# A four-layer graph network on one core: where layer 0's finished rows are split into word planes

## The chip, the core and the metric

The kernel runs on one core of a Trainium2 chip. A core has five instruction streams: PE (TensorE, matrix products; its weight loads are listed as PEld), DVE (VectorE), ACT (ScalarE), POOL (GpSimd) and SP (SyncE, which here only issues DMAs). Each executes its own list of instructions in order and waits on semaphores for the others. The metric is the device time of one launch in microseconds (us), lower is better. The time before the change is the median of three runs.

## The reference

A graph of 2708 nodes with 512 features goes through four layers; after each layer the result is added to its input and every row is normalised. The change touches layer 0 and the way from layer 0 to layer 1:

```python
x = _layernorm(x + _L0_gnn_ref(x, adj, W_nb, b_nb, W_line, b_line, 64))

# _L0_gnn_ref: mean over at most the first 64 neighbours of each node
keep = Ab & (jnp.cumsum(Ab.astype(jnp.int32), axis=1) <= neibor_num)
nb_mean = (keep.astype(X.dtype) @ X) / jnp.maximum(cnt, 1.0)
xj = leaky_relu(nb_mean @ W_nb.T + b_nb)
xi = leaky_relu(X @ W_line.T + b_line)
return xi + jnp.where(cnt > 0, xj, 0)
```

Layer 1 takes the finished rows x, multiplies them by two folded weight matrices and by the full adjacency. Layers 2 and 3 are graph attention; nothing of them is touched.

## The kernel before

The rows are handled in 22 tiles of 128 (the last, tile 21, has 20 rows; the name LAST). One work buffer for masks, `maskT`, holds the transposed adjacency of all tiles in a small format. Instructions of each engine are put in order at build time by a scheduler, which goes by the order in which the program creates them and by its own estimate of when each is ready; an instruction whose buffer is not yet free is put later. On the chip each engine keeps that order. The program ties some instructions behind others by hand (`issue_after`).

Layer 0 has two stages. In the first (to about 190 us in the profile) y = x W_nb is made for all tiles and kept on chip in two parts (yH, yL), and r0 = x W_line + b_line is written to DRAM (`r0_dram`). The second stage, the one that matters here, runs from about 190 to 486 us. It computes, block by block, the sums of neighbours keep @ y. A block is up to four row tiles; the blocks are taken in the order 20-21, 0-3, 4-7, 8-11, 12-15, 16-19 (`cuts`). For each block the loop goes over j = 0 to 21:

- `kept` (L470, ACT) makes `kT`, the slice of the mask for this j and this block, in two rotating buffers.
- L608 (PE) multiplies it with yH and yL of tile j, for each of the block's tiles: up to eight matmuls per j.
- `next(todo)` in two of three steps j runs one step of `finish` for the block before.
- `next(both)` in each step j runs one step of `other_masks`, and when that is used up of `weights1`, and then of `vectors`.

At the end of a block ACT scales its sums into `us` (L621).

`finish` has two steps per tile. The first fetches the tile's r0 and x (`fetched`, L205, issued by SP) and does on DVE: add a bias to u (L524), leaky (L229) on u and on r0, and r0 += x (L528). The second does on DVE u = u * has + r0 (L530) and the layer norm of u (L121 to L128, with one power on POOL, L126); then POOL stores the row tile to `x1_dram` (L532), and `store_words` (L149, L150) copies u once more, split into a plane of low and a plane of high 16-bit words, and POOL stores this copy to `x1_words`. In the next loop these words are read back by transposing DMAs (L155), tile by tile.

The fetched tiles lie in three rotating buffers with the name "rows" (pool `ahead`). The r0 and the x of a tile are two of them. The same three serve `weights1`, which fetches eight tiles of layer 1's weights, transposes them on PE (L139) between the sums and multiplies them (L299), and the transposing reads of the next loop. The memory for the word planes is the r0 tile itself, so its buffer is in use from the fetch of r0 until the store of the words has landed.

`other_masks` makes the last eight tiles of the mask. For each: a DMA of adjacency rows (L312, POOL), a count on ACT (L317), four running counts on DVE (`place`, L323 and L326), a transposing DMA on SP (`turn`, L344), and, some steps j later, signs on ACT into `maskT` (L349). These signs stand in ACT's list between kT instructions. Each mask takes 11 steps j.

The two rotating buffers with the name "u" (pool `sm`) hold r0 results in the first stage, and u results in the loop after this stage (L642). In this stage one of them is `acc`, a sum that `weights1` builds; the other has no use.

Of the kernel before, what the change touches and what calls it, by code (L numbers as in the profile page):

```python
# [10 lines left out]
F32 = mybir.dt.float32  # L11
# [9 lines left out]
P = 128  # L21
D = 512
# [10 lines left out]
def kernel(  # L33
# [18 lines left out]
    def rows(t):  # L52
        return min(P, N - t * P)
# [38 lines left out]
    x1_words = dram.tile([N, 2 * D], U16, name="x1_words")  # L92
# [51 lines left out]
    def store_words(room, dst, t, u):  # L144

        if t == LAST:
            return
        words = room.bitcast(U16)
        nc.vector.tensor_copy(words.rearrange("p (h c) -> p h c", h=2), u.bitcast(U16).rearrange("p (c h) -> p h c", h=2))  # L149
        nc.gpsimd.dma_start(dst[t * P:t * P + P, :], words)  # L150
# [86 lines left out]
    with ExitStack() as phase:  # L237
# [23 lines left out]
        sm = phase.enter_context(tc.tile_pool(name="l01", bufs=2))  # L261
# [44 lines left out]
        cuts = [(b, min(b + 4, NT)) for b in range(0, NT, 4)]  # L306
        cuts = cuts[-1:] + cuts[:-1]
# [48 lines left out]
        with ExitStack() as ph:  # L356
# [65 lines left out]
            for t in range(NT):  # L422
# [27 lines left out]
                u = sm.tile([P, D], F32, name="u")  # L450
# [12 lines left out]
        with ExitStack() as ph:  # L463
# [56 lines left out]
            def finish(ts_, us):  # L520
                for t in ts_:
                    n, u = rows(t), us[t]
                    r0, x0 = fetched(r0_dram, t, n), fetched(x, t, n)
                    nc.vector.tensor_add(u[:n], u[:n], b_nb[:n])  # L524
                    leaky(u[:n], u[:n])
                    with tc.issue_after(low.ins):
                        leaky(r0, r0)
                        nc.vector.tensor_add(r0, r0, x0)  # L528
                    yield
                    nc.vector.scalar_tensor_tensor(u[:n], u[:n], has[:n, t:t + 1], r0, op0=OP.mult, op1=OP.add)  # L530
                    layer_norm(sm, u[:n], n, u[:n])
                    nc.gpsimd.dma_start(x1_dram[t * P:t * P + n, :], u[:n])  # L532
                    store_words(r0, x1_words, t, u)
                    yield

            wnb, wself = [], weight2
            acc = sm.tile([P, D], F32, name="u")
            bias1 = sm.tile([P, D], F32, name="bias1", bufs=1)  # L540

            def weights1():
# [55 lines left out]
            for i, b in enumerate(cuts):  # L598
                ts_ = range(*b)
# [28 lines left out]
            for t in range(NT):  # L628
# [12 lines left out]
                u = sm.tile([P, D], F32, name="u")  # L641
# [3 lines left out]
        with ExitStack() as ph:  # L645
            st = ph.enter_context(tc.tile_pool(name="l1b", bufs=2))
            for t in range(NT):
# [12 lines left out]
                u = sm.tile([P, D], F32, name="u")  # L660
# [36 lines left out]
    cuts = [-((-NT * i) // nb) for i in range(nb + 1)]  # L697
# [938 lines left out]
```

## Time and profile before

| what | value |
|---|---|
| median of three runs | 2902.19 us (2900.64 to 2906.04) |
| the profiled execution's own time | 2901.7 us |
| its span in the profile | 2899.6 us |
| mean granted clock of PE | 0.994 |
| L608, sums of layer 0 with yH, busy | 173.4 us, 418 matmuls |
| L608, sums with yL, busy | 166.1 us, 418 matmuls |
| L866, DVE, attention weights, busy | 1132.1 us |
| L1067, PE, attention sums, busy | 894.2 us |

The profile is one execution taken by the hardware profiler. Its span runs from the first to the last recorded instruction; the execution's own time is 2.1 us longer. A line of a timeline has the start in us from the span's start, the duration in us, the engine, the line of the program, the operation, what it writes and reads with sizes, how often, and in brackets how long the engine stood idle before it and what released it. On SP the instruction's duration is that of issuing the DMA. Matmul ends are modelled, and neighbouring ones overlap; intervals between starts are more reliable than durations. A list of waits has the waiting engine and line, the one waited for, total us, times, and the longest.

### The profile page before, as it was taken

The numbers are of one execution on the slowest core, as the hardware profiler recorded it, in microseconds if no ns is written. First come the engines' busy times: TensorE is split into PE (matmuls) and PEld (weight loads), VectorE is DVE, ScalarE is ACT, GpSimd is POOL, SyncE is SP. The second block draws the span as 40 slices with busy tenths as digits, with TensorE's granted clock in tenths as the row PEclk, the third lists the DMA queues.
The fourth block names the chain that finished last, engine by engine and source line by source line (L and its number), as shares of the span: only waits on it lengthen the run. The fifth ranks groups of instructions, "written<-read, shape, count | busy, mean of one in ns | idle before, by whom it ended". The sixth has DMA issues, their size and how long they took to land. (4 is left out here: it accounts for less than half of the span.)

```text
span 2899.6 us, 35696 instructions
## 1 busy us (share of the span) xinstructions
PE 2810.6 (97%) x13910; PEld 1556.4 (54%) x13910; DVE 2009.6 (69%) x2386; ACT 1525.3 (53%) x1749; POOL 269.2 (9%) x436
## 2 busy tenths in 40 slices
PE   9999889999999999999999999999999999999998
PEld 5457666448887443444466433434475555555565
DVE  6867647644334999999978999999953535345343
ACT  4646533223234999999965999999951000000011
POOL 2112211101120000000012000000201010100001
PEclk9999999999999999999999999999999999999999
DMA  7745537524324011111143111110161000000000
GB/s 170 151 101 116 151 104 178 160 63 124 112 91 89 27 37 36 35 46 39 38 141 126 38 37 36 40 57 34 35 160 62 4 26 15 26 15 16 15 15 28
DMA packets 203669, 202.64 MB, mean 70 GB/s; under 512 B 126838, under 2 KB 151739, under 8 KB 203491
## 3 DMA queue, kind: packets, MB, share of 16 engines
q1 hardware_dynamic: 170646, 127.60, 16.7%
q0 software_dynamic: 21840, 68.46, 8.1%
q10 hardware_dynamic: 11004, 4.22, 0.6%
q8 instruction: 111, 1.82, 0.3%
q14 instruction: 68, 0.55, 0.1%
HBM read 137.90 MB, written 55.66 MB: 67 GB/s over the span
## 5 line engine op out<-in xcount | busy, mean ns | idle before, releaser
L866 DVE SCALAR_TENSOR_TENSOR e<-v_bc,ucol,maskT 128x1408 f32<-128x1408 f32 (+3 forms) x798 | 1132.1, 1484 | 316.8 <-PE pn L1267 308.3
L895 ACT ACTIVATE c<-e,bcol 128x1300 fp8e4<-128x1300 f32 (+2 forms) x688 | 956.7, 1412 | 61.5 <-DVE e L866 16.5
L1067 PE MATMUL po<-e,R 128*64 128x512 f32 (+3 forms) x4224 | 894.2, 548 | 25.7 <-DVE e L866 23.3
L1067 PEld LDWEIGHTS po<-e,R 128*64 128x64 f32 (+1 forms) x4224 | 333.7, 136 | 553.2 <-issue 389.7
L1267 PE MATMUL pn<-e,R 128*128 128x512 f32 (+1 forms) x1008 | 396.3, 557 | 0.8
L1267 PEld LDWEIGHTS pn<-e,R 128*128 128x128 f32 x1008 | 177.5, 190 | 195.9 <-issue 181.5
L1196 ACT ACTIVATE w<-pl,b 128x256 f32<-128x256 f32 (+1 forms) x88 | 41.0, 466 | 365.6 <-PE pl L1194 365.6
L608 PE MATMUL acc<-yH,kT 128*128 128x512 f32 x418 | 173.4, 415 | 15.5 <-ACT kT L470 14.2
L126 POOL TENSOR_TENSOR ln_rs<-ln_rs,half 128x1 f32<-128x1 f32 (+1 forms) x88 | 54.9, 624 | 1363.5 <-DVE ln_rs L125 1347.8
L787 PE MATMUL pm<-w,xT 128*128 128x264 f32 (+1 forms) x704 | 164.1, 388 | 2.8 <-issue 0.9
L608 PE MATMUL acc<-yL,kT 128*128 128x512 f32 x418 | 166.1, 397 | 0.0
L658 PE MATMUL acc<-yH,mf 128*128 128x512 f32 x418 | 162.7, 389 | 0.0
L658 PE MATMUL acc<-yL,mf 128*128 128x512 f32 x418 | 162.6, 389 | 0.0
L1194 PE MATMUL pl<-lin 128*128 128x256 f32 (+1 forms) x704 | 152.9, 371 | 0.6 <-DVE lin L1096 0.6
L1219 PE MATMUL pl<-lin,w 128*128 128x512 f32 x336 | 150.8, 593 | 0.0
L1194 PEld LDWEIGHTS pl<-lin 128*128 128x128 f32 x704 | 129.3, 190 | 31.2 <-issue 15.8
L787 PEld LDWEIGHTS pm<-w,xT 128*128 128x128 f32 (+1 forms) x704 | 129.7, 190 | 28.6 <-ACT xT L141 3.1
L655 ACT CAST mf<-maskT 128x1024 fp32r<-128x1024 fp8e4 (+1 forms) x66 | 64.5, 978 | 149.0 <-PE acc L658 144.4
L299 PE MATMUL pm<-w,xT 128*128 128x512 f32 x288 | 130.0, 594 | 1.6 <-DVE yL L276 1.0
L470 ACT ACTIVATE kT<-maskT 128x512 fp32r<-128x512 fp8e4 (+1 forms) x132 | 77.3, 592 | 100.4 <-PE acc L608 100.1
L967 PE MATMUL pd<-c,parts_c 128*12 128x384 fp8e4 (+2 forms) x2688 | 128.3, 307 | 0.0
L299 PE MATMUL pm<-weight,xT 128*128 128x512 f32 (+1 forms) x256 | 117.4, 602 | 2.6 <-DVE u L642 2.6
(278 smaller groups left out, 2780.1 us busy)
## 6 DMA issues: line engine op xcount, KB each, us to landing
v_bc<-v_dram SPq DMA_DIRECT2D x16, 704.0 KB
rows<-in_x_dram SPq DMA_DIRECT2D x42, 256.0 KB
x_dram<-u POOLq DMA_DIRECT2D x42, 256.0 KB, 2.4
v_bc<-v_dram SPq DMA_DIRECT2D x16, 650.0 KB
m<-in_adj_dram POOLq DMA_DIRECT2D x13, 677.0 KB, 7.8
r_dram<-u POOLq DMA_DIRECT2D x21, 256.0 KB, 3.6
rows<-r_dram SPq DMA_DIRECT2D x21, 256.0 KB
x_words<-rows POOLq DMA_DIRECT2D x21, 256.0 KB, 3.6
```

Of the source, the lines that this page charges most:

```text
L299: order(nc.tensor.matmul(pm[:m], xT[:, k, :m], w[:, k, :], start=(k == 0), stop=(k == KD - 1)))
L470: made = nc.scalar.activation(kT[:, :w], maskT[:, j, b[0] * P:b[0] * P + w], AF.Relu, scale=-1.0)
L608: nc.tensor.matmul(pa[t], kT[:, (t - b[0]) * P:(t - b[0] + 1) * P], y(j), start=(j == 0 and y is yH), stop=(j == LAST))
L658: nc.tensor.matmul(pa, mf[:, j - g0, :], y(j), start=(j == 0 and y is yH), stop=(j == LAST))
L787: nc.tensor.matmul(pm[a][:m, :D // 2 + heads], xT[:, k, :m], w[:, k, a, :D // 2 + heads], start=(k == 0), stop=(k == KD - 1))
L866: self.made = nc.vector.scalar_tensor_tensor(e[:, :w], v[:, :w], ucol[:, j, h:h + 1], maskT[:, j, c0:c0 + w], op0=OP.max, op1=OP.mult)
L895: nc.scalar.activation(c[:, :w], e[:, :w], AF.Sigmoid, bias=bcol[:, j, h:h + 1], scale=STEP, saturate=False)
L967: pe(nc.tensor.matmul(p[32 * g:32 * g + 12, :c1 - c0], parts_c[:, j, h, :], c[:, c0:c1], start=(i == 0 and h == hs[0]), stop=(i == NT - 1 ...
L1067: pe(nc.tensor.matmul(po[i][HO * k:HO * k + HO, :c1 - c0], R2[at, j, h * HO:(h + 1) * HO], e[at, a:a + c1 - c0], start=(i_ == 0), stop=(i_ ...
L1194: nc.tensor.matmul(pl[:, :w], self.lin1[:, k, f * P:(f + 1) * P], h[:, k, :w], start=(k == 0), stop=(k == KD - 1))
L1219: nc.tensor.matmul(pl[:n], gT[:, f, (t - t0) * P:(t - t0) * P + n], self.lin2[:, f, :], start=(f == 0), stop=(f == KF - 1))
L1267: nc.tensor.matmul(pn[k][:, :w], R2[at, j, k * P:(k + 1) * P], e[at, :w], start=(j == 0), stop=(j == NT - 1))
```

## The change

Two lines are edited. A second tile of the name "u" is taken beside `acc` for the whole stage, `words`. `finish` gives it to `store_words` as the place for the word planes, except for the tiles of the last block (16 to 19), which are finished in the loop after this stage and still use r0's own memory. So 17 tiles (20 and 0 to 15) share one buffer for their words; tile 21 has no words.

```diff
@@ finish
                     layer_norm(sm, u[:n], n, u[:n])
                     nc.gpsimd.dma_start(x1_dram[t * P:t * P + n, :], u[:n])
-                    store_words(r0, x1_words, t, u)
+                    store_words(r0 if ts_ == range(*cuts[-1]) else words, x1_words, t, u)
                     yield
...
             wnb, wself = [], weight2
-            acc = sm.tile([P, D], F32, name="u")
+            acc, words = (sm.tile([P, D], F32, name="u") for _ in range(2))
             bias1 = sm.tile([P, D], F32, name="bias1", bufs=1)
```

`store_words` itself, unchanged:

```python
words = room.bitcast(U16)
nc.vector.tensor_copy(words.rearrange("p (h c) -> p h c", h=2), u.bitcast(U16).rearrange("p (c h) -> p h c", h=2))
nc.gpsimd.dma_start(dst[t * P:t * P + P, :], words)
```

## The prediction

> **What bounds the kernel now.** I read the page first, for the engine that sets the span, then the waits of TensorE (PE) inside the one stage that the change touches, then backwards along the queues that cause those waits: ScalarE (ACT), SP, VectorE (DVE), SP again. From the page, busy us and share by engine:
>
> ```profile
> PE 2810.6 (97%) x13910; PEld 1556.4 (54%) x13910; DVE 2009.6 (69%) x2386; ACT 1525.3 (53%) x1749; POOL 269.2 (9%) x436
> ```
>
> From the list of PE's waits between 222 and 490 us (waiting engine and line, who was waited for, us in total, times, longest):
>
> ```profile
> PE acc L608 <- ACT kT L470: 18.0, 12, 6.8
> PE ps_tr L139 <- DMA rows<-in_L_gnn_W_self_dram: 4.8, 1, 4.8
> PE acc L608 <- ACT u L621: 1.3, 2, 0.6
> ```
>
> PE is busy 97% of the span, so time is won only where PE stands still. In this stage (the masked sums of layer 0) it stands still for about 24 us. PE's timeline names the long gaps (start, duration, instruction, idle time before it and releaser):
>
> ```profile
> 324.65 0.80 PE L608 MATMUL acc<-yH,kT 128*128 128x512 f32 x1 [3.34 <-ACT kT L470]
> ...
> 353.75 5.28 PE L608 MATMUL acc<-end,kT 128*128 128x512 f32 x12 [6.78 <-ACT kT L470]
> ...
> 375.58 0.68 PE L608 MATMUL acc<-yH,kT 128*128 128x512 f32 x1 [3.10 <-ACT kT L470]
> ...
> 391.36 1.12 PE L139 MATMUL ps_tr<-ident,rows 128*128 128x128 f32 x4 [4.82 <-DMA rows<-in_L_gnn_W_self_dram]
> ```
>
> I call them A, B, C and D: 3.34 + 6.78 + 3.10 + 4.82 = 18.04 us. After each of them PE is also slow for a while. The table by stretch gives length, busy time of PE, PEld, DVE, ACT and POOL, and then the granted clock (PEclk): 0.54 after A, 0.69 after B, and 1.00 in a quiet stretch after D:
>
> ```profile
> 324.60:328.20 3.60, 3.54 (x9) 2.83 (x10) 2.76 (x6) 2.10 (x4) 2.53 (x4) 0.54 0.91 135
> 353.70:361.80 8.10, 8.00 (x22) 5.48 (x23) 4.22 (x8) 5.90 (x11) 0.53 (x1) 0.69 0.53 183
> ...
> 400.00:408.00 8.00, 8.00 (x32) 5.24 (x31) 0.00 (x0) 2.50 (x5) 0.00 (x0) 1.00 0.14 43
> ```
>
> Matmuls of this stage start 0.227 us apart in undisturbed stretches. After A, 8 intervals took 3.46 us instead of 1.81 (1.65 lost); after B, 22 took 8.13 instead of 4.99 (3.14 lost); after C, 10 took 3.97 instead of 2.27 (1.70 lost); after D, four transposes, eight sums and eight product matmuls took 7.62 us against 5.33 for the same group ten microseconds later (2.29 lost). Together 8.8 us, so the four gaps cost 26.8 us.
>
> Why are they there? A, B and C wait for kT, which ACT makes; ACT's timeline shows it stuck, ahead of kT, on a mask transpose that arrives late:
>
> ```profile
> 352.12 1.06 ACT L349 ACTIVATE maskT<-weight 128x1024 fp8e4<-128x1024 bf16 x1 [8.60 <-DMA weight<-spare]
> ```
>
> That is B; the same instruction waited 5.15 us before A and 4.36 us before C. The transposes (L344) left SP at 317.85, 346.20 and 368.68 us, each within 0.2 us of DVE's last L326 on that mask. So DVE's scans of the mask were late, and DVE's timeline shows why, here before A:
>
> ```profile
> 301.07 0.69 DVE L528 TENSOR_TENSOR rows<-rows 128x512 f32<-128x512 f32 x1 [4.52 <-DMA rows<-in_x_dram]
> 307.17 0.69 DVE L229 SCALAR_TENSOR_TENSOR rows<-rows 128x512 f32<-128x512 f32 x1 [5.41 <-DMA rows<-r_dram]
> 307.89 0.69 DVE L528 TENSOR_TENSOR rows<-rows 128x512 f32<-128x512 f32 x1
> 308.50 1.56 DVE L323 TENSOR_TENSOR_SCAN w<-w,over 128x677 bf16<-128x677 bf16 x1
> ```
>
> The scan (L323) of a mask that had been counted by 295 us begins at 308.50, behind two row fetches. And the fetches were late because SP could not issue them. The longest entry of SP's waits between 183 and 560 us, and one fetch on its timeline:
>
> ```profile
> SPq L205 <- DMA x_words<-rows: 67.2, 16, 12.6
> ...
> 331.57 0.33 SPq L205 DMA_DIRECT2D rows<-in_x_dram  x1
> ```
>
> POOL sent tile 4's words store at 327.29; SP's next fetch goes at 331.57, when that store has landed. The circle is closed: a "rows" buffer is held until the words made in it are in DRAM, the fetch into it goes late, DVE stands, the scan, the transpose, the sign and kT are late, PE stands.
>
> **What the Trainium skill says.** "TensorE: Matmul & The Clock Gate", section "HAM oscillation — how this bites in real kernels": idle gaps of more than about 3.4 us drop PE to half clock. The trace agrees: 0.43 us between matmuls instead of 0.227 after A, B and C, even after C's 3.10 us. "Perfetto Trace Analysis", section "DMA Instruction — SWDGE (GPSIMD)": the profiled end of such a DMA is the end of descriptor generation, not of the movement. The trace agrees: a words store occupies POOL for 0.54 us and lands 3.5 us after its issue (median between 300 and 390 us) or 5.2 us (between 183 and 300). "Perfetto Trace Analysis", section "Optimization Strategy": a repeated bubble on the engine that should be saturated can mean that there are too few buffers for the next tile; A to C repeat once per mask and end in a buffer wait.
>
> **The change part by part.** (1) The copy L149 stays one DVE instruction of 0.68 us; only its destination differs, for tile 20 and tiles 0 to 15 (17 copies). The store on POOL and its bytes stay. Cost 0. The buffer was the idle second one of "u" until the next loop's first u at 493 us, about 30 us after tile 15's words left POOL (462.24). Cost 0.
>
> (2) A row buffer comes free after L530, not after the store has landed. For tile 2, L530 ends at 283.1, while the words left POOL at 290.48 and landed 3.5 to 5.2 us later: 11 to 13 us earlier. For tile 3 it is 292.6 against 296.85 + 4.3 = 301.1. For tile 0 it is 265.4 against 278.53. So the waits of DVE at L528 and L229 shrink: 5.16 + 4.52 + 5.41 us between 276 and 308, 3.72 + 4.39 + 3.63 us between 330 and 359.
>
> (3) A new wait: with one buffer, the copy of a tile must wait until the tile before's words have landed. Of the four copies of a block only the first two stand close, 270.84 and 273.16 (and 326.11 and 328.43); the next is 16.0 and 6.7 us later (13.7 and 6.7). The first store is issued at 272.02; landed after 3.5 to 6.5 us, the second copy starts at 275.5 to 278.5, so it waits 2.4 to 5.4 us; I take 4. The third and fourth wait for 0 to 2; I take 0. Behind the waiting copy on DVE stand the scans of the next mask, and behind those SP's transpose, ACT's signs and PE. On POOL the words store waits with the copy, and the next power (L126) or mask load behind it by as much.
>
> Now the gaps. A: its mask's scans start after about 10 us of fetch waits (4.52 + 5.41); those gone, the transpose leaves some 8 us or more earlier, and ACT's wait was 5.15. A goes: 3.34 + 1.65 = 5.0. C is the same case one block later (4.39 + 3.63 against 4.36 on ACT): 3.10 + 1.70 = 4.8. D: the W_self fetch left SP at 388.70, when L528 of tile 11 was done; tile 10's and 11's rows move up by about 9 us (tile 10's second fetch, at 381.09, waited for tile 8's store; L530 of tile 8 ends near 371.6). PE needed the tile at 386.5. D goes: 4.82 + 2.29 = 7.1.
>
> B is the tight one. Its mask shares DVE with the finishing of four tiles. A deadline can be read from the block before: it starts at 261.49, its transpose leaves at 293.21 and costs PE 0.52 us, so 293.21 - 0.52 - 261.49 = 31.2 us after a block's start is early enough. B's block starts at 303.74; DVE's work from 317.63 to 346.05 is 28.4 us with 3.72 of fetch wait in it, so 24.7 without. It can begin 0.9 us after the block's start, as it does in the block before (the last L326 ends at 262.39). 0.9 + 24.7 + the words wait of 2.4 to 5.4 = 28 to 31 us, just inside. I leave 3 us of B's 9.9 standing (2 of idle, 1 of slow clock), since nothing is spare: 6.9 gained.
>
> Sum: 5.0 + 6.9 + 4.8 + 7.1 = 23.8 us. Everything after 490 us is PE-bound with its own order and moves up as a whole. The span was 2899.6 us; the profiled execution's own time, 2901.7, lies 2.1 around it and 0.5 below the median 2902.19. 2902.2 - 23.8 = 2878.4 us.
>
> **The rivals.** (a) The new wait takes half back: copies wait 5 to 6 us per block ahead of a scan, B stays (9.9) and C comes back in part (2): gain 12, 2890 us. For: only 0 to 3 us spare in B's block. Against: 15.1 and 11.7 us of DVE waits go. Chance 0.12. (b) Nothing to be measured: the order on the engines was laid out around the old waits, and ACT's signs stay late for another reason, for instance a transpose queued on SP behind a row fetch that waits for L530. L344 at 262.52 and the end of L530 at 265.4 are only 3 us apart. Gain 0 to 5, 2900 us. Chance 0.09. (c) Slower: three copies per block each stand a whole landing of 6.5 us ahead of the scans, 19.5 us against the 15.1 and 11.7 removed. Then scans are later than before by 4.4 and 7.8 us, PE idles by these 12.2, and about 4 of slow clock follow: 2918 us. It decides from the point where the words waits of a block exceed some 12 to 15 us. Against it: two of the three spacings are 6.7 us or more. Chance 0.08. (d) More: B goes whole (3) and the two waits of 1.79 and 1.17 us at 465 and 470, where x1's first transposed words (SP, 457.70) are late on ACT, go too, since tiles 12 to 15 finish sooner: gain 30, 2872 us. Chance 0.16.
>
> **How the numbers follow.** The forecast has 0.55 (gain 18 to 28, 2874 to 2884), (a) 0.12, (b) 0.09, (c) 0.08, (d) 0.16. About 0.2% (5.8 us) is what a measurement of this kernel can tell from no change. Faster: 0.55 + 0.12 + 0.16 = 0.83; same 0.09; slower 0.08. The range runs from 2869 (all of A to D, the 3 us of late words and their slow clock) to 2898 (a gain of 4); (c), part of (b) and a little beyond (d) are left out, together not quite 2 in 10.
>
> **What would show it.** In the new profile SP's wait for the words store is gone from L205; DVE's waits at L528 and L229 in 262 to 360 us fall from 26.8 us to under 10; ACT no longer waits for the transposes by more than 2 us; PE's gaps A, C and D are absent, and PEclk stays near 1.0 from 305 to 432 us. A new line shows DVE's L149 waiting for the words DMA, some 2 to 5 us per block. I am wrong if that wait is over 12 us per block, if the transposes on SP stand behind a fetch, or if PE still waits for kT with the fetches on time.

## The result, and the profile after

The changed kernel takes 2885.65 us (median of 5 runs, 2884.27 to 2889.62); beside it on the same chip the kernel before takes 2904.49 us (2900.64 to 2906.83). The ratio is 0.9939, with a 95% interval from 0.9924 to 0.9953: 18.8 us less, where 23.8 were forecast, at the lower edge of the forecast's own band of gains (18 to 28). The profiled execution took 2884.27 us, with a span of 2882.5; the spans differ by 17.1 us.

PE is as much the engine that sets the time as before (busy us, share of the span, instructions, from the page of the changed kernel):

```profile
PE 2806.0 (97%) x13910; PEld 1553.3 (54%) x13910; DVE 2008.4 (70%) x2386; ACT 1525.4 (53%) x1749; POOL 267.1 (9%) x436
```

The list of PE's waits between 222 and 490 us has lost over 60% of the waiting for kT (18.0 us before) and the whole of the waiting for W_self (the L299 waits belong to the loop after this stage, 2.30 us of them at 489.35):

```profile
PE acc L608 <- ACT kT L470: 6.8, 8, 3.3
PE pm L299 <- DVE yL L276: 2.7, 2, 2.3
PE pm L568 <- ACT w L560: 1.7, 1, 1.7
PE acc L608 <- ACT u L621: 0.9, 2, 0.6
```

PE's timeline shows what is left of the long gaps. There are two, and they are not both leftovers: the first is in a block that had none of over 0.6 us before.

```profile
300.33 4.61 PE L608 MATMUL acc<-end,kT 128*128 128x512 f32 x12 [2.23 <-ACT kT L470]
...
346.53 5.49 PE L608 MATMUL acc<-end,kT 128*128 128x512 f32 x12 [3.30 <-ACT kT L470]
```

A clean account uses no busy times, only the start of L621, with which ACT ends each block's sums. Us from one such start to the next:

| stretch | before | after | gain | forecast |
|---|---|---|---|---|
| start to first L621 | 220.49 | 219.06 | 1.43 | 0 |
| sums of tiles 0 to 3 | 40.29 | 40.30 | -0.01 | 0 |
| sums of tiles 4 to 7 | 42.25 | 45.08 | -2.83 | 0 |
| sums of tiles 8 to 11 | 55.34 | 46.70 | 8.64 | 11.9 (A and B) |
| sums of tiles 12 to 15 | 71.99 | 59.70 | 12.29 | 11.9 (C and D) |
| sums of tiles 16 to 19 | 55.34 | 53.74 | 1.60 | 0 |
| from there to the end of the span | 2413.90 | 2417.92 | -4.02 | 0 |

The five blocks of sums together went from 265.21 to 245.52 us: 19.7 us gained. The first and the last row of the table are not explained by the change. In the profiled executions of the experiments below, the first row lies between 217.9 and 221.6 us and the last between 2412.7 and 2418.5. Both kernels' values lie in these spreads, so I read both rows as scatter of single executions. The first row goes with the granted clock, whose mean up to the first L621 is 0.98 before and 0.99 after. The 4.0 us of the last row consist of 1.66 in the loop that follows (to the first L658), 1.12 from the first to the last L1067 and 1.07 from there to the first L1267, where the profile of the changed kernel has a spell of slow clock that the kernel before has not. Only the 1.66 us could belong to the change: 155.97 us is the shortest that this loop takes in any profile, though e6, which keeps the words in r0 as well, has 158.19. No experiment isolates it.

Now the chain backwards, as the prediction went. ACT's timeline shows the two mask transposes that are still late, one for each gap:

```profile
298.70 1.06 ACT L349 ACTIVATE maskT<-weight 128x1024 fp8e4<-128x1024 bf16 x1 [4.05 <-DMA weight<-spare]
...
344.90 1.06 ACT L349 ACTIVATE maskT<-weight 128x1024 fp8e4<-128x1024 bf16 x1 [5.12 <-DMA weight<-spare]
```

SP's waits between 183 and 560 us: the wait for the words store (67.2 us before) is down to 9.1, all of it after the last sums, in the loop where r0's own memory is still used. The three lines together:

```profile
SPq L205 <- DVE rows L528: 32.8, 14, 7.7
...
SPq L205 <- DVE u L530: 12.6, 11, 2.7
...
SPq L205 <- DMA x_words<-rows: 9.1, 3, 4.9
```

The fetches are now released by DVE's own arithmetic (L528 and L530), as the change intends. And DVE's timeline, within the sums of tiles 4 to 7 (259 to 304 us):

```profile
277.28 0.69 DVE L149 COPY u<-u 128x1024 uint16<-128x1024 uint16 x1 [3.60 <-DMA x_words<-u]
...
279.22 1.56 DVE L323 TENSOR_TENSOR_SCAN spare<-spare,over 128x677 bf16<-128x677 bf16 x1
...
292.48 0.69 DVE L528 TENSOR_TENSOR rows<-rows 128x512 f32<-128x512 f32 x1
299.17 0.69 DVE L229 SCALAR_TENSOR_TENSOR rows<-rows 128x512 f32<-128x512 f32 x1 [6.00 <-DMA rows<-r_dram]
299.77 1.56 DVE L323 TENSOR_TENSOR_SCAN w<-w,over 128x677 bf16<-128x677 bf16 x1
```

Two waits stand ahead of mask scans. The first is the new one: a copy that waits for the words of the tile before to land, 3.60 us here, and behind it the scans of one mask (`spare`). The second is an old acquaintance: a row of r0 that is not there, 6.00 us, and behind it the scans of the next mask (`w`). SP's timeline shows when that row was asked for:

```profile
291.40 3.39 SPq L344 DMA_TRANSPOSE weight<-spare  x1
294.89 1.19 SPq L205 DMA_DIRECT2D rows<-r_dram  x1
```

Its buffer came free at 293.17, when L528 had ended (292.48 + 0.69). SP was then still issuing the transpose, until 294.79, and sent the fetch 0.1 us later; 4.3 us after that it was there. So of the 6.00 us, 1.7 are time behind the transpose and 4.3 the landing.

The transpose itself, sent at 291.40, was there for ACT at 298.70: a landing of 7.30 us, where the same one took 5.24 in the kernel before, from these two lines of its SP and ACT timelines:

```profile
293.21 3.28 SPq L344 DMA_TRANSPOSE weight<-spare  x1
...
298.45 1.06 ACT L349 ACTIVATE maskT<-weight 128x1024 fp8e4<-128x1024 bf16 x1 [2.33 <-DMA weight<-spare]
```

"Landing" here is always the time from SP's issue to ACT's first sign, which in each case quoted is waiting for it. POOL's timeline of the changed kernel shows what was sent meanwhile, the row and the words of tile 3:

```profile
292.14 0.59 POOL L532 DMA_DIRECT2D x_dram<-u  x1 [0.89 <-DVE u L128]
292.87 0.54 POOL L150 DMA_DIRECT2D x_words<-u  x1
```

In the kernel before, a pair of such stores left 4.1 and 2.7 us ahead of this transpose and the next pair 2.9 and 3.6 us behind it. B's transpose stood between stores in the same way and landed in 5.93 us (346.20 to 352.12; 6.00 and 5.94 in e1 and e9), so some 0.7 us of landing vary for a reason that no run here shows.

### The profile page after: what moved, and what is told of

Read it like the earlier page. It is cut to its first block, busy times and chain, and to the rows that moved or that the text cites. A ratio compares the mean times of both kernels' runs of the same rounds, so it can differ in the third digit from the quotient of the medians.

```text
span 2882.5 us, 35707 instructions
## 1 busy us (share of the span) xinstructions
PE 2806.0 (97%) x13910; PEld 1553.3 (54%) x13910; DVE 2008.4 (70%) x2386; ACT 1525.4 (53%) x1749; POOL 267.1 (9%) x436
## 5 line engine op out<-in xcount | busy, mean ns | idle before, releaser
L1067 PE MATMUL po<-e,R 128*64 128x512 f32 (+3 forms) x4224 | 894.0, 548 | 25.4 <-DVE e L866 23.1
L1067 PEld LDWEIGHTS po<-e,R 128*64 128x64 f32 (+1 forms) x4224 | 333.9, 136 | 552.5 <-issue 389.4
L1267 PE MATMUL pn<-e,R 128*128 128x512 f32 (+1 forms) x1008 | 396.3, 557 | 0.7
L1267 PEld LDWEIGHTS pn<-e,R 128*128 128x128 f32 x1008 | 177.5, 190 | 195.9 <-issue 181.2
L658 PE MATMUL acc<-yH,mf 128*128 128x512 f32 x418 | 162.7, 389 | 0.0
L658 PE MATMUL acc<-yL,mf 128*128 128x512 f32 x418 | 162.6, 389 | 0.0
L1194 PEld LDWEIGHTS pl<-lin 128*128 128x128 f32 x704 | 129.3, 190 | 31.2 <-issue 15.8
L299 PE MATMUL pm<-w,xT 128*128 128x512 f32 x288 | 130.1, 594 | 3.5 <-DVE yL L276 2.7
L299 PE MATMUL pm<-weight,xT 128*128 128x512 f32 (+1 forms) x256 | 117.1, 600 | 1.5 <-DVE u L642 1.5
```

What stands on the lines that cost most here:

```text
L299: order(nc.tensor.matmul(pm[:m], xT[:, k, :m], w[:, k, :], start=(k == 0), stop=(k == KD - 1)))
L658: nc.tensor.matmul(pa, mf[:, j - g0, :], y(j), start=(j == 0 and y is yH), stop=(j == LAST))
L1067: pe(nc.tensor.matmul(po[i][HO * k:HO * k + HO, :c1 - c0], R2[at, j, h * HO:(h + 1) * HO], e[at, a:a + c1 - c0], start=(i_ == 0), stop=(i_ ...
L1194: nc.tensor.matmul(pl[:, :w], self.lin1[:, k, f * P:(f + 1) * P], h[:, k, :w], start=(k == 0), stop=(k == KD - 1))
L1267: nc.tensor.matmul(pn[k][:, :w], R2[at, j, k * P:(k + 1) * P], e[at, :w], start=(j == 0), stop=(j == NT - 1))
```

## The experiments

The theory: the gain comes from the time at which a row buffer is released; what is missing against the forecast is (i) the wait of the copies for the single words buffer, (ii) the row fetch that DVE meets ahead of the scans and, a part added after these had been tried, (iii) the slower landing of the transpose. The rivals: the gain comes from something else in the change (another memory, another order on the engines); the rest is missing because of the order in which scans and finishing steps are taken, or because the signs stand too early in ACT's list. All results at once; "blocks" is the time from the first to the last start of L621, which takes in the five blocks and leaves out what lies before and after them. Each ratio is to the kernel before in the same round (medians 2902.02 to 2904.56), so rounds are better compared by ratio than by median:

| kernel | median us | ratio to before, interval | blocks us |
|---|---|---|---|
| before | 2904.49 | | 265.2 |
| after | 2885.65 | 0.9939 (0.9924 to 0.9953) | 245.5 |
| e1_hold | 2909.60 | 1.0014 (1.0008 to 1.0021) | 269.6 |
| e2_two_planes | 2878.07 | 0.9910 (0.9895 to 0.9925) | 239.6 |
| e3_scan_first | 2882.83 | 0.9921 (0.9909 to 0.9934) | 245.5 |
| e4_not_12_15 | 2885.28 | 0.9930 (0.9916 to 0.9944) | 247.2 |
| e5_late_signs | 2888.78 | 0.9950 (0.9937 to 0.9964) | 249.2 |
| e6_before_late | 2903.41 | 0.9998 (0.9989 to 1.0007) | 267.8 |
| e7_guard | 2878.33 | 0.9910 (0.9895 to 0.9926) | 235.7 |
| e8_both | 2876.68 | 0.9911 (0.9895 to 0.9926) | 238.5 |
| e9_late_tiles | 2897.44 | 0.9978 (0.9970 to 0.9985) | 257.2 |
| e10_early_tiles | 2892.13 | 0.9962 (0.9949 to 0.9975) | 252.8 |
| e11_all_words | 2888.45 | 0.9955 (0.9943 to 0.9967) | 244.9 |
| e12_later_store | 2881.57 | 0.9926 (0.9912 to 0.9940) | 242.6 |

### Does the release time of the row buffer carry the gain? (e1_hold)

Everything of the change stays, but a small second DMA reads 64 bytes per row of r0 behind the words store, so that the row buffer is in use about as long as before.

```diff
-        nc.gpsimd.dma_start(dst[t * P:t * P + P, :], words)
+        return nc.gpsimd.dma_start(dst[t * P:t * P + P, :], words)
...
+                    sent = store_words(r0 if last else words, x1_words, t, u)
+                    if sent is not None and not last:
+                        with tc.issue_after(sent.ins):
+                            nc.gpsimd.dma_start(hold_dram[t * P:t * P + n, :], r0[:, :16])
```

> The changed kernel, with one small DMA more per tile on POOL (64 bytes of each r0 row to a scratch tensor, sent right behind the words store), so that r0's row buffer stays in use until about the landing of the words, as before the change; the words still lie in their own buffer. Theory (the gain comes from row buffers that come free earlier): the gain goes, the old row-fetch waits of DVE return and the new wait for the words stays: 2900 to 2912 us, and PE's gaps of 3 to 7 us before 400 us return. Rival (the gain comes from another order of the instructions on the engines, not from the release): 2884 to 2890 us, as the changed kernel.

The gain is gone, and the kernel is 5.0 us slower than before (2909.60 against 2904.56 beside it). SP's list of waits has the old wait under a new name, and PE's timeline has A, B and C back (line numbers are up by one to five in this kernel):

```profile
SPq L206 <- DMA hold_dram<-rows: 55.5, 11, 13.0
```

```profile
323.97 0.79 PE L613 MATMUL acc<-yH,kT 128*128 128x512 f32 x1 [3.62 <-ACT kT L471]
...
352.80 4.74 PE L613 MATMUL acc<-end,kT 128*128 128x512 f32 x12 [5.66 <-ACT kT L471]
...
375.12 0.79 PE L613 MATMUL acc<-yH,kT 128*128 128x512 f32 x1 [3.57 <-ACT kT L471]
```

D is back too, 5.12 us at 392.09. With the words in their own buffer and only the release late, nothing is gained; so it is the release time, and not where the words lie. The added DMAs are a change of their own, but e9 and e10 below, which add none, place the gaps where the release time says. The extra 5 us are not split further between the 17 added DMAs and a hold that is somewhat longer than before.

### Which tiles carry which gap? (e9_late_tiles, e10_early_tiles)

The change for one half of the tiles alone:

```diff
-                    store_words(r0 if ts_ == range(*cuts[-1]) else words, x1_words, t, u)
+                    store_words(words if 8 <= t < 16 else r0, x1_words, t, u)          # e9
+                    store_words(words if t < 8 or t == 20 else r0, x1_words, t, u)     # e10
```

> The change for tiles 8 to 15 alone; tiles 20 and 0 to 7 split their words in r0 again. Theory (each gap belongs to the row buffers of the tiles that are finished in the same block, so the parts stand by themselves): the sums of tiles 4 to 7 and 8 to 11 are as before (42 and 55 us, gaps A and B there), the sums of tiles 12 to 15 start late with C but lose D, 72 us become 62 to 68, the rest as in the changed kernel; gain 5 to 10 us, 2894 to 2899. Rival (D follows from the lateness that the blocks before hand on): with A and B there D stays too, at most 3 us smaller; gain under 4, 2900 or more. Second rival (the late tiles carry C and D alone): sums of tiles 12 to 15 at 60 us, gain 12 or more.

> The change for tiles 20 and 0 to 7 alone; tiles 8 to 15 split their words in r0 again. Theory (each gap belongs to the row buffers of the tiles finished in the same block): sums of tiles 4 to 7 at 45 us and of tiles 8 to 11 at 47 us as in the changed kernel, C gone, D back in the sums of tiles 12 to 15, which take 64 to 68 us; gain 6 to 12 us, 2892 to 2898. Rival (D follows from lateness handed on): D stays away too and the sums of tiles 12 to 15 take 60 us as in the changed kernel, gain 15 or more, 2889 or less.

Both as the theory has it. With the late tiles alone, PE's timeline keeps A, B and C; D is gone:

```profile
324.13 0.50 PE L608 MATMUL acc<-yH,kT 128*128 128x512 f32 x1 [3.59 <-ACT kT L470]
...
353.78 5.49 PE L608 MATMUL acc<-end,kT 128*128 128x512 f32 x12 [7.29 <-ACT kT L470]
...
375.72 0.50 PE L608 MATMUL acc<-yH,kT 128*128 128x512 f32 x1 [3.19 <-ACT kT L470]
```

With the early tiles alone, the two gaps of the changed kernel are there (2.16 us at 301.81 and 4.01 at 348.02), C is gone and D is back:

```profile
348.02 4.39 PE L608 MATMUL acc<-end,kT 128*128 128x512 f32 x12 [4.01 <-ACT kT L470]
...
378.95 1.12 PE L139 MATMUL ps_tr<-ident,rows 128*128 128x128 f32 x4 [3.46 <-DMA rows<-in_L_gnn_W_self_dram]
```

The sums of tiles 12 to 15 take 64.75 and 64.67 us, between 71.99 and 59.70. The two gains, 7.2 and 7.3 us, come to more than the 12.3 of both together: with C gone D is smaller, 3.46 us instead of 4.82, so the two are not quite independent. Over all blocks the halves nearly add up: 8.0 + 12.4 us against 19.7 for both. Little lateness is handed from block to block.

### Is the wait for the single words buffer what is missing? (e2_two_planes)

A second place for the words, so that tiles 1, 3, 5 and 7 don't share one with their neighbours; it is a buffer of the next loop (`xT`), unused in this stage. (A third row-sized buffer of its own was not tried, nor a fourth row buffer.)

```diff
+            second = ahead.tile([P, KD, P], F32, name="xT").rearrange("p k n -> p (k n)")
...
-                    store_words(r0 if ts_ == range(*cuts[-1]) else words, x1_words, t, u)
+                    store_words(r0 if ts_ == range(*cuts[-1]) else second if t < 8 and t % 2 else words, x1_words, t, u)
```

> The changed kernel, with a second buffer for the words of tiles 1, 3, 5 and 7 (one of the two xT buffers, idle there), so that the copies of tiles 0 to 7 need not wait for the tile before. Theory (the new wait of DVE for the words, 3.60 and 2.34 us, is what leaves PE's gaps of 2.23 us at 300 and 3.30 us at 346 standing): the waits and both gaps go with their slow clock, the sums of tiles 4 to 7 and of 8 to 11 take about 41 us each instead of 45.1 and 46.7: 2876 to 2880 us. Rival (the gaps come from transposes that take 7.2 us instead of 5.2 to 5.9 beside stores sent at the same time, or from DVE's load): the waits go, the gaps stay within 1 us, 2883 to 2888 us.

The time is what the theory gave. DVE's waits between 222 and 380 us: the words wait is 1.2 us instead of 7.2, the one for rows of r0 stays (12.6 in the changed kernel):

```profile
DVE rows L229 <- DMA rows<-r_dram: 12.3, 3, 5.9
...
DVE u L149 <- DMA x_words<-u: 1.2, 1, 1.2
```

The sums of tiles 4 to 7 come down from 45.08 to 41.34 us, the first gap is gone. The sums of tiles 8 to 11 come down only from 46.70 to 45.25 instead of to 41: the second gap stays, with 2.89 us of idle time. So removing the wait pays, and it was not the whole. Nor is it one thing that went: without the wait the last two stores of a block also leave ahead of the transpose (287.60 and 289.71 against 289.99), which lands in 5.73 us; e12 takes that part by itself.

### Is the row fetch ahead of the scans the other part? (e7_guard)

Built on e2. L229 on r0 of each block's third tile is tied behind the scans before it, so DVE no longer meets the missing row ahead of a mask (`placed`, set where a scan is made, holds the last of them).

```diff
-                    with tc.issue_after(low.ins):
+                    third = placed and t == ts_[2 if len(ts_) > 2 else 0] and t < 12
+                    with tc.issue_after(low.ins), tc.issue_after(placed[0].ins) if third else nullcontext():
                         leaky(r0, r0)
```

> The kernel with two planes buffers (tiles 1, 3, 5, 7 in xT's), and on DVE the leaky of r0 of each block's third tile tied behind the scans of the mask before it, so that DVE does not wait for that fetch (5.9 us, the fetch stands behind a transpose on SP) with scans behind it. Theory (the gap of 2.89 us at 342 us is left by this wait): the scans of the block's second mask start 4 to 6 us earlier, the gap goes, the sums of tiles 8 to 11 take 41 to 42 us instead of 45.3: 2873 to 2876 us. Rival (the gap comes from DVE's load within the block): the gap stays within 1 us, 2876 to 2880 us.

In the trace it is exactly so. ACT, at the place of the second gap, hardly waits for the transpose:

```profile
339.11 1.06 ACT L349 ACTIVATE maskT<-weight 128x1024 fp8e4<-128x1024 bf16 x1 [0.49 <-DMA weight<-spare]
```

DVE's waits between 222 and 380 us have no line for L229 any more; what stands first is a wait for the count of a mask, so the scans are now early enough to wait for ACT:

```profile
DVE w L323 <- ACT w L317: 14.1, 3, 8.3
DVE rows L529 <- DMA rows<-in_x_dram: 6.6, 3, 4.2
```

The sums of tiles 4 to 7 and 8 to 11 take 41.41 and 41.43 us, without a gap above 0.7 us, and the blocks together 235.7 us. The median is no better than e2's, though, and misses the expectation: the profiled execution took 2873.66 us, but of the six runs two lie at 2872.0 and 2873.7 and four between 2878.2 and 2881.0. The two short ones have a mean granted clock of 0.998 and 0.999, the four others 0.996 to 0.997, so what these lose goes with the clock. Only one execution has a profile, so where they lose it stays open.

### Do the stores delay the transpose? (e12_later_store)

The changed kernel, with the two stores of tile 3 moved on POOL behind the next mask load (L312), which waits until the transpose has landed. Tile 7's stores, one block on, keep their place in the trace (0.7 and 1.5 us behind the transpose, as in the changed kernel): they are the control.

```diff
-                    nc.gpsimd.dma_start(x1_dram[t * P:t * P + n, :], u[:n])
-                    store_words(r0 if ts_ == range(*cuts[-1]) else words, x1_words, t, u)
+                    later = t in (3, 7)
+                    if not later:
+                        nc.gpsimd.dma_start(x1_dram[t * P:t * P + n, :], u[:n])
+                    send = store_words(r0 if ts_ == range(*cuts[-1]) else words, x1_words, t, u, later)
                     yield
+                    if later:
+                        for _ in range(3):
+                            yield
+                        with tc.issue_after(roomed[0].ins):
+                            nc.gpsimd.dma_start(x1_dram[t * P:t * P + n, :], u[:n])
+                            send()
```

> The changed kernel, with the two row stores of tile 3 (x1 and words) moved on POOL behind the next mask load, which itself waits for the landing of the mask transpose; in the changed kernel both leave within 1.5 us after the transpose's start. Tile 7's stores keep their place, and are the control. Theory (the two stores delay the transpose that lands beside them): in the sums of tiles 4 to 7 the transpose lands in 5.2 to 5.9 us instead of 7.30, leaving SP as late as before (32.0 us after the last L621), PE's gap there falls from 2.23 to 0.9 us or less and this block takes 41.5 to 43 us instead of 45.08; in the sums of tiles 8 to 11 it lands in 6.9 to 7.3 us as before and its gap stays near 3.3; median 2881 to 2885. Rival (the row fetch that SP sends behind the transpose, or something else, delays it): landing 6.9 to 7.3 us in both, gap 2.0 to 2.4 us, this block 45 us, median as in the changed kernel or, by the store's later landing, above it.

The theory holds, against the rival of the row fetch as well, which still follows the transpose on SP. The two transposes on SP's timeline and their first signs on ACT's, the treated one first:

```profile
292.63 3.36 SPq L347 DMA_TRANSPOSE weight<-spare  x1
296.08 0.54 SPq L206 DMA_DIRECT2D rows<-r_dram  x1
...
337.69 3.37 SPq L347 DMA_TRANSPOSE weight<-spare  x1
```

```profile
297.81 1.06 ACT L352 ACTIVATE maskT<-weight 128x1024 fp8e4<-128x1024 bf16 x1 [2.06 <-DMA weight<-spare]
...
344.92 1.06 ACT L352 ACTIVATE maskT<-weight 128x1024 fp8e4<-128x1024 bf16 x1 [0.81 <-DMA weight<-spare]
```

5.18 us with the stores out of the way, 7.23 with them beside it (297.81 - 292.63 and 344.92 - 337.69). PE's gap in the first block is down to 0.27 us, and the block takes 41.94 us. The store that was moved takes its toll elsewhere: it holds the tile's u until it has landed, and the last of ACT's four L621 waits for that:

```profile
308.17 0.69 ACT L634 ACTIVATE u<-acc,rkeep 128x512 f32<-128x512 f32 x1 [3.98 <-DMA x_dram<-u]
```

PE stands still for 3.94 us behind it, until 308.91, and the next block takes 47.77 us against 46.70 in the changed kernel. A third of this block's gain of 3.14 us is given back there, and that block cannot be compared. The median is 20.5 us below that of the kernel before beside it (2902.02), against 18.8 for the changed kernel; the intervals overlap.

With this, the gaps in these two blocks can be followed from the transpose to PE. In the table, "left" is the time from the start of the block before's L621 to the transpose on SP, "landing" from there to ACT's first sign:

| kernel, sums of tiles | left | landing | sum | sum - 37.15 | PE idle |
|---|---|---|---|---|---|
| before, 4 to 7 | 32.43 | 5.24 | 37.67 | 0.52 | 0.52 |
| after, 4 to 7 | 32.04 | 7.30 | 39.34 | 2.19 | 2.23 |
| after, 8 to 11 | 33.24 | 7.22 | 40.46 | 3.31 | 3.30 |
| e2, 4 to 7 | 30.73 | 5.73 | 36.46 | below 0 | none |
| e2, 8 to 11 | 34.19 | 5.77 | 39.96 | 2.81 | 2.89 |
| e3, 4 to 7 | 32.19 | 6.91 | 39.10 | 1.95 | 1.95 |
| e3, 8 to 11 | 34.22 | 7.24 | 41.46 | 4.31 | 4.32 |
| e7, 4 to 7 | 30.42 | 5.71 | 36.13 | below 0 | none |
| e7, 8 to 11 | 29.96 | 5.87 | 35.83 | below 0 | none |
| e10, 8 to 11 | 33.91 | 7.19 | 41.10 | 3.95 | 4.01 |
| e12, 4 to 7 | 32.18 | 5.18 | 37.36 | 0.21 | 0.27 |

The 37.15 is fixed by the first row alone; the other rows then come out within 0.1 us, and so do e4 and e11, which are not printed. What this shows is that the time of ACT's first sign alone sets PE's gap in these blocks. It holds where nothing else keeps PE waiting, so not in e5, e6 and e8, nor in the sums of tiles 8 to 11 of the kernel before, e1 and e9. That the landing follows the stores is shown by e12, not by the sum; across the other runs it is 7.19 to 7.30 us with the stores 0.7 and 1.5 us behind the transpose, and 6.68 to 6.91 with them 1.2 and 1.9 us behind.

### Is it the order of scans and finishing steps? (e3_scan_first)

```diff
-                    if j % 3:
-                        next(todo, None)
                     with tc.issue_after(nxt_made.ins):
                         next(both, None)
+                    if j % 3:
+                        next(todo, None)
```

> The changed kernel, with the step of the mask, of the weights or of the vectors created before the step of finish in each j, so that scans go ahead of row finishing on DVE. Theory (scans are late because DVE does other work first): the transposes leave SP 2 to 4 us earlier in a block, PE's two gaps shrink to under 1 us: 2876 to 2882 us. Rival (they are late by landing, beside stores): gaps within 1 us of the changed kernel, 2883 to 2888 us.

It is not: both gaps stay (1.95 us at 301.54, 4.32 at 348.27), and the blocks take 245.5 us as in the changed kernel. Its median is 2.8 us lower, within what the intervals leave open.

### Do the signs stand too early in ACT's list? (e5_late_signs, e6_before_late, e8_both)

The signs of a mask are put two steps j later in the changed kernel (e5), four steps later in the kernel before (e6), and two steps later together with e7 (e8). The core of it, as in e5:

```diff
                         place(i, m, places, part, 4)
-                        next(left, None)
+                        if part > 1:
+                            next(left, None)
                         yield
+                    for _ in range(2):
+                        next(left, None)
+                        yield
                     for _ in left:
                         pass
-                    yield
-                    yield
                     turn(i, m, into)
```

> The changed kernel, with the signs of each mask created two steps j (3.6 us) later, between the scans' last two steps and the next transpose, and nothing else moved. Theory (PE waits only because the signs of masks that are needed much later stand in ACT's list ahead of kT): ACT no longer waits for a transpose by more than 3 us, PE's gaps at 300 and 346 us go or fall under 1 us, although the transposes leave SP as late as before: sums of tiles 4 to 7 and 8 to 11 in 41 to 43 us each, 2876 to 2880 us. Rival (PE is short of something else in these blocks, for instance DVE's or the DMA engines' share): gaps stay, 2883 to 2888 us.

> The kernel before, with its words in r0's memory, and the signs of each mask created four steps j (7.2 us) later. Theory (the row fetches cost time only through late scans, late transposes and the signs in ACT's list): DVE still waits over 20 us for row fetches between 262 and 360 us, but PE's gaps A and B (3.34 and 6.78 us) go or fall under 1 us, C may stay in part; D (the W_self fetch, which needs a row buffer) stays at 4 to 5 us: 2884 to 2892 us. Rival (late rows hold PE by another way): A, B and C stay, 2900 to 2908 us.

> Two planes buffers, the third tile's leaky behind the scans, and the signs two steps later. Theory: no gap over 1 us is left in the sums of tiles 0 to 15; the sums of tiles 8 to 11 take 40 to 41 us: 2872 to 2875 us, at most 3 us better than the guard alone. Rival: the later signs delay the next transposes, which need the same buffer, and the gaps come back later: 2878 us or more.

All three missed what was expected. In e5 the gap of the first block goes but for 1.40 us at its end, but all masks go through one buffer, so a transpose may not start before the signs of the mask before have been read: the transposes leave SP at 312.68, 339.46 and 360.48 us instead of 308.66, 337.68 and 354.92, row fetches stand behind them, and a larger gap opens at the start of a block (and one of 2.56 us at 368.35, in the sums of tiles 12 to 15, which take 66.32 us), on PE's timeline:

```profile
350.28 0.80 PE L610 MATMUL acc<-yH,kT 128*128 128x512 f32 x1 [5.84 <-ACT u L623]
```

In e6 gap A goes, and another instruction in ACT's list takes its place, the count of a mask whose adjacency rows come late, since their load leaves POOL at 329.28 us, behind the stores of two tiles, where it left ahead of them at 323.61 in the kernel before:

```profile
338.84 2.55 ACT L317 ACTIVATE w<-w,gate 128x2708 bf16<-128x2708 bf16 x1 [6.17 <-DMA w<-in_adj_dram]
```

PE then waits 6.49 us until 342.06; at B's place PE waits 2.27 us instead of 6.78, but at C's 6.47 instead of 3.10 (until 374.51), and nothing is gained (0.9998). So in the kernel before it was not one instruction in ACT's list that was late: moving one step along the line of the masks moves the gap. On top of e7 (e8) the later signs change the median by 1.7 us, less than the intervals tell apart; gaps of 1.40 us open at the start of three blocks, and the blocks take 238.5 us, 2.8 more than in e7.

### What are the tiles left out worth? (e4_not_12_15, e11_all_words)

```diff
-                    store_words(r0 if ts_ == range(*cuts[-1]) else words, x1_words, t, u)
+                    store_words(r0 if ts_ in (range(*cuts[-1]), range(*cuts[-2])) else words, x1_words, t, u)   # e4
+                    store_words(words, x1_words, t, u)                                                          # e11
```

> The changed kernel, with the words of tiles 12 to 15 again in r0's own memory. Theory (the 4 us that the next loop lost come from the reads of x1's words that now stand ahead of the loads for the attention vectors on SP): the sums of tiles 16 to 19 take again 55 us instead of 53.7, the loop after them is some 4 us shorter: 2880 to 2884 us. Rival (the loss in the loop is due to something else): no shorter loop, 2886 to 2889 us.

> The changed kernel, with the words buffer for tiles 16 to 19 as well, which are finished in the loop after this stage. Theory (that loop's row fetches wait for words stores too, 9.1 us of SP waits in three goes are left in the changed kernel, but its PE bound absorbs most): within 3 us of the changed kernel, 2883 to 2889; SP's waits for the words store from r0 are gone. Rival (the buffer is the loop's second u buffer, so the loop's u results, which then come one at a time, hold PE up): 2890 or more, with PE waiting for DVE or ACT on u at L642 and after. Second rival (the rows that come free earlier are worth something): 2880 or less.

In e4 the sums of tiles 16 to 19 take 55.1 us again (55.34 before, 53.74 after): the 1.6 us in the table above belong to the words of tiles 12 to 15. The loop that follows does not become shorter in exchange (150.5 us from its first to its last L271, 150.7 in the changed kernel), so that part of the theory fell; the median, 2885.28 us, lies between what the theory and its rival gave. In e11 the median is 2.8 us above the changed kernel's, with overlapping intervals; SP's wait for the words store from r0 is gone, and on PE's timeline the wait at the start of the loop, 2.30 us in the changed kernel, has grown:

```profile
492.40 5.40 PE L299 MATMUL pm<-w,xT 128*128 128x512 f32 x8 [4.28 <-DVE yL L276]
```

So extending the buffer's life to the last tiles gains nothing, although the SP wait that it removes is real.

## Why the prediction was right, point by point

**The circle (right, shown).** A words store held the row buffer, and the release time carried the gain: e1 puts the release back and the gain is gone, with the same waits under a new name. This is the case of which the Trainium skill speaks in "Perfetto Trace Analysis", section "Optimization Strategy": a bubble that repeats on the saturated engine may come from too few buffers. Here it was not their number but how long one of them was held.

**C and D (right in size).** 11.9 us forecast, 12.29 measured in the sums of tiles 12 to 15; e9 and e10 show D to go with the words of tiles 8 to 15 and C with those of the early tiles, as the prediction derived them from two different fetches; it added them as independent, while D turned out to depend in part on C.

**A (right) and B (mis-sized).** A is gone. Of B's 9.9 us, 3 were to stay. The sums of tiles 8 to 11 take 46.70 us; without any gap they take 41.43 (e7), so 5.3 are left, 3.30 of them idle. The prediction saw that this mask was "just inside" its deadline of 31.2 us after the block's start, at 28 to 31. Of its idle 3.30 us, the table gives 0.81 to a transpose that left later than its model (33.24 against 32.43 us) and 1.98 to its landing (7.22 against 5.24), over the model's own 0.52. Counted as the prediction counts, from the block's start at 305.15, it left after 32.5 us, above the 28 to 31 that were worked out. They let this mask's work begin 0.9 us after the block's start; it began after 3.4 (308.52), since the 6.00 us of waiting for a row in the block before had pushed the mask ahead of it (its transpose left at 308.66). e7 removes that wait. Of the landing's 1.98 us, 0.7 were in the kernel before already, where B's transpose took 5.93.

**The new words wait (right as a line, its reach mis-sized).** Taken at 4 us once per block, bounds 2.4 to 5.4; measured 3.60, 2.34, 1.26 and 1.08, one to a block, all but the first below the bounds. Rival (c), three full landings per block, is out. The forecast charged it to B alone; what it costs is in two places. e2, which takes the wait away and with it the stores behind the transpose, gains 3.74 us in the sums of tiles 4 to 7 and 1.45 in those of 8 to 11.

**The deadline (the step that failed).** "31.2 us after a block's start is early enough" was read from the sums of tiles 4 to 7 in the kernel before, and their own transpose was counted as unchanged. It was: in the changed kernel it leaves even 0.39 us earlier in its block. But a deadline for leaving holds only with the landing that went with it, 5.24 us, and in the changed kernel the last stores of a block leave right behind the transpose, where they had left well ahead of it and well behind it. The landing became 7.30 us, the block lost 2.83 us that the forecast had at nothing, and B's block had the same long landing (7.22) on top of a transpose that left late. e12 shows this part by itself: the stores away, 5.18 us and no gap.

**The waits of DVE for rows (half right).** They were to fall from 26.8 us to under 10 between 262 and 360 us. They fell to 12.0, all of it two waits for r0 (L229). In the longer list from 222 to 380 us the waits for x (L528) fell from 19.3 to 6.0 us, those for r0 (L229) from 13.6 to 12.6, in three waits as before. The prediction's step 2 treated both alike, as fetches that wait for a words store. After the change, the fetch of r0 waits for another release, L528 of a row before it, and then for SP, which is busy issuing a transpose for 3.39 us. e7, which on top of e2 lets DVE pass that wait, empties both blocks of gaps. Accordingly "ACT no longer waits for the transposes by more than 2 us" did not come true (4.05 and 5.12), while "the transposes on SP stand behind a fetch", named as a way to be wrong, was the other way round: a fetch stood behind a transpose. Nor did the granted clock stay near 1.0 up to 432 us: it was 0.79 and 0.65 after the two gaps.

**The account.** Forecast 23.8 us; in the blocks 19.7: 2.83 lost in the sums of tiles 4 to 7, 3.26 less in those of 8 to 11, against 0.4 more in 12 to 15 and 1.6 in 16 to 19 (part of rival (d)). 23.8 - 2.83 - 3.26 + 0.4 + 1.6 = 19.7. The medians say 18.8. The two misses are largely of one kind: about 2 us of landing in each of two blocks, and PE's slow clock after the gaps that they cause; in B's block 0.8 us of late departure come to it. The gain in 16 to 19, which the forecast did not count on though rival (d) did, hides 1.6 us of them in the total; so far the nearness of the total is luck.

**A better version.** e2, e7 and e8, with a second place for the words, have medians of 2876.68 to 2878.33 us. The runs of e7 (2872.0 to 2881.0) and e8 (2873.1 to 2880.7) do not overlap with the changed kernel's (2884.3 to 2889.6), taken in another round; one of e2's does. Among the three the measurement doesn't choose.

## What to carry to other kernels

Scratch data that leaves by DMA should not lie in a buffer that another queue is waiting to refill: the buffer's release is then the landing of the store, not the end of the last arithmetic on it, and one wait can come back as a repeated gap three engines further on. When such a buffer is separated, the new buffer is itself a rotating one with its own landing to wait for; count its uses against that landing, and check the new wait against every stage that runs at its edge, not only against the one that is late now. A deadline read from a trace is one for the landing of a transfer, not for its issue: before it is used elsewhere, look at what else the queues send in the same microseconds.

## What the runs showed of the hardware

- Gaps shorter than those before can slow PE, but need not. The table by stretch of the changed kernel (length, busy time of PE, PEld, DVE, ACT, POOL, then the granted clock) has the time after each of the two gaps, after a gap of 2.30 us in the next loop, and a quiet stretch:

```profile
300.30:308.40 8.10, 7.86 (x24) 5.37 (x25) 7.86 (x8) 6.33 (x11) 0.53 (x1) 0.79 0.51 88
346.50:354.60 8.10, 8.07 (x22) 5.61 (x23) 8.00 (x14) 5.90 (x11) 0.53 (x1) 0.65 0.34 116
489.30:497.40 8.10, 7.94 (x18) 3.44 (x19) 5.91 (x10) 1.43 (x2) 0.54 (x1) 1.00 0.85 268
400.00:408.00 8.00, 8.00 (x31) 5.12 (x30) 0.94 (x2) 2.34 (x5) 0.00 (x0) 1.00 0.13 35
```

24 and 22 matmuls in 8.1 us against 31 in 8.0, at a clock of 0.79 and 0.65, after idle times of 2.23 and 3.30 us; after 2.30 us the clock stayed at 1.00. Over the 14 profiles, between 225 and 640 us, no idle time of PE up to 1.85 us was followed by a lower clock, 15 of the 22 from 1.95 to 3.03 us were, and all 24 from 3.10 us on. The clock was then at half for 3.4 us or more, up to 6.7. The Trainium skill, "TensorE: Matmul & The Clock Gate", section "HAM oscillation — how this bites in real kernels", puts the loss at gaps of more than about 3.4 us; here shorter ones cost it too. The prediction took its trace to agree with that figure, although A (3.34 us) and C (3.10) were already below it.

- A transposing DMA is slowed by ordinary row stores that are sent just behind it. From SP's issue to ACT's first sign: 7.30 and 7.22 us in the changed kernel, 5.18 with the two stores moved away (e12) and 7.23 in its control; 5.71 to 5.87 with the stores sent up to 2.4 us ahead of it (e2, e7). What the two share, queue or memory, no run here tells.
- SP is taken for 3.3 to 4.4 us by issuing one such transpose (5.70 once, in e8), and whatever stands behind it in SP's list waits for that: 1.7 of the 6.00 us for the row in the changed kernel.
